# Layer 1 of a two-layer attention mixer on one core: from a scheduled loop to steps in a written order, with the range checks inside it

## The chip, the cores and the metric

The kernel runs on one core of a Trainium2 chip, in one launch. The metric is the device time of a run in microseconds (us). The profile shows one execution: its span runs from the first to the last instruction. The engines are TensorE (PE: matmuls and transposes, with weight loads as PEld), VectorE (DVE), ScalarE (ACT), GpSimd (POOL) and SyncE (SP, which issues the DMAs). They run side by side and wait for each other by semaphores. Matmuls write to PSUM[...]; ACT and DVE read them out from there, which is called evacuating a bank.

## What is computed

The input x has 128 rows of 256 tokens with 256 channels, all float32. Two layers each add an attention to x. In front of each stands a group norm over all rows. Layer 1 is the one that changes:

```
x2 = gn(x).reshape(rows, F=256, C=256)           # 128 rows
q, k, v = split(x2 @ w_in.T + b_in)              # 4 heads of 64
scores = q k^T / 8, kept where |i - j| <= 16     # a band
out = softmax(scores) v
x = x + out @ w_out.T + b_out
```

Layer 0 is an attention without a band, with 8 heads, a bias computed from z, and a gate. The fast path of the kernel leaves out the maximum in the softmax. So at the end it checks that what it relied on lies in safe ranges (the exponentials of the bias, the reciprocal sums of both layers, the mask). One number, the verdict, then decides whether a second, general path has to run. With these inputs it does not.

## The kernel before

The kernel (`fast_kernel`) works in four stages: it loads weights and z and computes the bias exponentials `eb` and the moments of x; layer 0 over 64 pairs of rows (its last output row is multiplied at about 2219 us); layer 1 over the same 64 pairs; and the checks.

Layer 1 treats a pair `p` as follows. `prep1` loads its rows (`xt`, 512 KB), adds the output bias into a second tile `xb` on POOL, transposes `xt` on PE (L1537) into PSUM and evacuates it by ACT to `xgT`. Then come four projections of 128 output channels each, two for q and two for k (L1546, evacuated by ACT), and the values of the two rows (L1560, evacuated by a DVE add). `scores1` makes the scores of one row (L1585): only the band is computed, in blocks of 64 keys by 96 queries, and these small matmuls use 64 by 64 parts of the PE array[...]. ACT takes their exponential into `e`, and POOL multiplies `e` by the band mask in two halves (L1595). `apply1` multiplies with the values and sums up with ones (L1612), in 64 by 32 parts of the array, into the four fixed banks `o_eo` and `su_eo`. Even and odd key blocks go to different banks. Two ACT copies, three DVE adds and products and a DVE reciprocal (L1617 to L1623) join them into the normalized `oT`. `finish1` multiplies by `w_out` (L1630), and a DVE add with `xb` writes the row to `yo` (L1634). At the second row of a pair `yo` goes out, and the reciprocal sums `rv` go to DRAM (`rsum1`).

All PSUM tiles of transposes, projections, values and output rows share one tag, `mm`, with two banks; the scores have one tile of two banks. Which of the two `mm` banks a tile gets is settled when the program is built.

The order of the work in layer 1 is that of a scheduler. The loop offers the work of pair `p` and, through a generator, pieces of the preparation of pair `p + 1`; the scheduler orders the instructions by its own estimates when the program is built. Layer 0 is different: there a `manual_schedule` block takes the instructions in the order in which the code issues them.

After layer 1 the checks run (L943 to L948, called from L1684 on). `check` makes three DVE passes over a tile: greater than a lower bound, less than an upper one, and a minimum. It is called for `eb` (4096 elements per partition), for the sums of layer 0 (2048) and of layer 1 (1024), both read back from DRAM, and for the mask (256). A matmul over the four results gives the verdict.

Of the kernel before, what the change touches and what calls it, by code (L numbers as in the profile page):

```python
# [9 lines left out]
F32 = mybir.dt.float32  # L10
# [763 lines left out]
def fast_kernel(  # L774
# [164 lines left out]
    ok = const.tile([P, 4], F32, name="ok")  # L939
    nc.vector.memset(ok, 1.0)  # L940

    def check(src, lo, hi, col, pool):

        n, m = src.shape
        a = pool.tile([n, m], F32, name="chk", tag="chk", bufs=1)
        nc.vector.tensor_scalar(a, src, lo, None, ALU.is_gt)
        nc.vector.scalar_tensor_tensor(a, src, hi, a, ALU.is_lt, ALU.mult)
        nc.vector.tensor_reduce(ok[:n, col : col + 1], a, AX.X, ALU.min)  # L948
# [555 lines left out]
    DH = P // H1  # L1504
    rsum1 = dram.tile([NP, H1, 2, I], F32, name="rsum1")
    with tc.tile_pool(name="l1", bufs=2) as sb, tc.tile_pool(
# [19 lines left out]
        def prep1(p, d):  # L1526
            s0 = 2 * p
            xt = sb.tile([P, 2 * NB, C], F32, name="xt1", tag="xt", bufs=3)
            nc.sync.dma_start(xt, rows(x1[s0 // GB], s0 % GB, 2))
            xb = sb.tile([P, 2 * NB, C], F32, name="xb1", tag="xb", bufs=3)  # L1530
            nc.gpsimd.tensor_tensor(xb, xt, bcast(bout_r, 1, 2 * NB), ALU.add)  # L1531
            d["xb"] = xb
            xgT = sb.tile([P, KC, N2], F32, name="xgT1", tag="xgT")
            for k in range(KC):
                ps = mm1("ps_x1")
                for t in range(2 * NB):
                    nc.tensor.transpose(ps[:, t * P : (t + 1) * P], xt[:, t, k * P : (k + 1) * P], ident)  # L1537
                nc.scalar.activation(xgT[:, k, :], ps, AF.Identity, bias=nM1[:, k : k + 1])  # L1538
            yield
            qT = sb.tile([P, KC, N2], F32, name="qT1", tag="qT")  # L1540
            kT = sb.tile([P, KC, N2], F32, name="kT1", tag="kT")
            for n, dst in ((0, qT), (1, kT)):
                for m in range(KC):
                    ps = mm1("ps_p1")
                    for k in range(KC):
                        nc.tensor.matmul(  # L1546
                            ps, w_in[:, k, n * C + m * P : n * C + (m + 1) * P], xgT[:, k, :],
                            start=(k == 0), stop=(k == KC - 1),
                        )
                    nc.scalar.activation(  # L1550
                        dst[:, m, :], ps, AF.Identity, bias=bin_c[:, n * KC + m : n * KC + m + 1]
                    )
                    yield
            v = sb.tile([P, 2, NB, C], F32, name="v1", tag="v")
            for r in range(2):
                ps = mm1("ps_v1")
                for b in range(NB):
                    t = r * NB + b
                    for k in range(KC):
                        nc.tensor.matmul(  # L1560
                            ps[:, b * C : (b + 1) * C], xgT[:, k, t * P : (t + 1) * P], w_in[:, k, 2 * C : 3 * C],
                            start=(k == 0), stop=(k == KC - 1),
                        )
                nc.vector.tensor_tensor(  # L1564
                    v[:, r, :, :], ps.rearrange("p (b c) -> p b c", b=NB), bcast(bv1_r, 1, NB), ALU.add
                )
                yield
            d.update(qT=qT, kT=kT, v=v)

# [7 lines left out]
        def scores1(d, r):  # L1577

            ps = ps_s.tile([P, 2, 512], F32, name="ps_sc1", tag="s")
            at = lambda q, c, j: ps[:, q, (c * 2 + j) * W : (c * 2 + j + 1) * W]  # L1580
            for c in range(KC):
                for k in range(NK):
                    for q in range(2):
                        rs = slice(q * D1, (q + 1) * D1)
                        nc.tensor.matmul(  # L1585
                            at(q, c, k // 2)[half(k)],
                            d["kT"][rs, c, r * I + k * KB : r * I + (k + 1) * KB],
                            d["qT"][rs, c, r * I + q0(k) : r * I + q0(k) + W],
                            start=True, stop=True,
                        )  # L1590
            e = sm.tile([P, 2, KC, NK // 2 * W], F32, name="e1", tag="e", bufs=3)
            ev = e.rearrange("p q c w -> p q (c w)")
            nc.scalar.activation(ev, ps[:, :, : KC * NK // 2 * W], AF.Exp)  # L1593
            for q in range(2):
                nc.gpsimd.tensor_tensor(  # L1595
                    e[:, q], e[:, q], bcast(bw.rearrange("p b w -> p (b w)"), 1, KC), ALU.mult
                )
            return e

        def apply1(d, r, e):  # L1600


            for a in range(3):
                for j in range(NK // 2):
                    for h in range(H1):
                        for k in (2 * j, 2 * j + 1):
                            at = slice(h * DH, (h + 1) * DH)
                            n = k % 2
                            to = o_eo[n][at, a, q0(k) : q0(k) + W] if a < 2 else su_eo[n][at, q0(k) : q0(k) + W]
                            w = (d["v"][half(k), r, j, h * D1 + a * DH : h * D1 + (a + 1) * DH] if a < 2  # L1610
                                 else ones[half(k), :DH])
                            nc.tensor.matmul(  # L1612
                                to, w, e[half(k), h % 2, h // 2, j * W : (j + 1) * W], start=True, stop=True,
                            )
            rv = d["rv"]
            odd = sm.tile([P, 3, I], F32, name="odd1", tag="odd", bufs=2)
            nc.scalar.copy(odd[:, 2, :], su_eo[1])  # L1617
            nc.scalar.copy(odd[:, :2, :], o_eo[1])  # L1618
            nc.vector.tensor_tensor(odd[:, 2, :], su_eo[0], odd[:, 2, :], ALU.add)
            nc.vector.reciprocal(rv[:, r, :], odd[:, 2, :])  # L1620
            nc.vector.tensor_tensor(odd[:, :2, :], o_eo[0], odd[:, :2, :], ALU.add)  # L1621
            oT = sb.tile([P, 2, I], F32, name="oT1", tag="oT", bufs=3)
            nc.vector.tensor_tensor(oT, odd[:, :2, :], bcast(rv[:, r, :], 1, 2), ALU.mult)  # L1623
            return oT

        def finish1(d, r, oT, yo):
            ps = mm1("ps_y1")
            for b in range(NB):
                for k in range(KC):
                    nc.tensor.matmul(  # L1630
                        ps[:, b * C : (b + 1) * C], oT[:, k, b * P : (b + 1) * P], w_out[:, k, :],
                        start=(k == 0), stop=(k == KC - 1),
                    )
            nc.vector.tensor_tensor(  # L1634
                yo[:, r * NB : (r + 1) * NB, :], ps.rearrange("p (b c) -> p b c", b=NB),
                d["xb"][:, r * NB : (r + 1) * NB, :], ALU.add,
            )

        todo1, ends1 = [], []

        def back1():
            d_, r_, es_ = todo1.pop(0)
            ends1.append((d_, r_, apply1(d_, r_, es_)))

        def end_row1():
            d_, r_, oT_ = ends1.pop(0)
            if r_ == 0:
                d_["yo"] = sb.tile([P, 2 * NB, C], F32, name="yo", tag="yo")
            finish1(d_, r_, oT_, d_["yo"])
            if r_ == 1:  # L1650
                p_ = d_["p"]
                nc.sync.dma_start(rows(out, 2 * p_, 2), d_["yo"])
                nc.sync.dma_start(
                    rsum1[p_].rearrange("q r i -> q (r i)"), d_["rv"][0:P:DH].rearrange("q r i -> q (r i)")
                )

        d = {}
        for _ in prep1(0, d):
            pass
        for p in range(NP):  # L1660
            nxt = {}
            ahead = prep1(p + 1, nxt) if p + 1 < NP else iter(())
            d.update(p=p, rv=sb.tile([P, 2, I], F32, name="rv1", tag="rv", bufs=3))
            for r in range(2):
                es = scores1(d, r)
                next(ahead, None)
                next(ahead, None)
                late = bool(ends1)
                if todo1:
                    back1()  # L1670
                next(ahead, None)
                if late:
                    end_row1()
                next(ahead, None)
                todo1.append((d, r, es))
# [87 lines left out]
```

## Time and profile before

| | us |
|---|---|
| median of three runs | 3584.51 (3583.58 to 3585.43) |
| profiled execution, whole | 3581.69 |
| its span | 3579.1 |
| first transposes of layer 1 on PE | 2241.7 |
| last out row added on DVE | 3545.6 |
| verdict written | 3571.98 |

Busy in the 200 us from 2600 on, in the middle of layer 1: PE 199.4, weight loads 132.8, DVE 92.4, ACT 70.5, POOL 59.9. The granted PE clock is full there (1.00), and the DMA engines are busy for 17%.

How to read it: a row of the timeline has the start of a group of equal instructions, its length, the engine, the line, the operation, what it writes and reads, and how many there are. The recorded end of a matmul is modelled and reaches past the start of the next one. So the price of a block of matmuls is read from the distance between the starts of two blocks. One float32 matmul shows as two records. A remark in brackets at the end of a row tells how long the engine was idle before it, and what ended this.

### The profile page before, as it was taken

The numbers are of one execution on the slowest core, as the hardware profiler recorded it, in microseconds if no ns is written. First come the engines' busy times: TensorE is split into PE (matmuls) and PEld (weight loads), VectorE is DVE, ScalarE is ACT, GpSimd is POOL, SyncE is SP. The second block draws the span as 40 slices with busy tenths as digits, with TensorE's granted clock in tenths as the row PEclk, the third lists the DMA queues.
The fourth block names the chain that finished last, engine by engine and source line by source line (L and its number), as shares of the span: only waits on it lengthen the run. The fifth ranks groups of instructions, "written<-read, shape, count | busy, mean of one in ns | idle before, by whom it ended". The sixth has DMA issues, their size and how long they took to land.

```text
span 3579.1 us, 80651 instructions
## 1 busy us (share of the span) xinstructions
PE 3355.8 (94%) x35154; PEld 2054.8 (57%) x35154; DVE 2086.4 (58%) x3412; ACT 1373.0 (38%) x1937; POOL 1812.9 (51%) x1257
## 2 busy tenths in 40 slices
PE   5666999999999999999999997999999999999995
PEld 3333555555555555555555554566666666666664
DVE  5864666666666666666666665344444444444445
ACT  2333444444444444444444442333333333333332
POOL 2355666666666666666666663223232332323221
PEclk8778999999999999999999998999999999999998
DMA  9961122212221222122212221111111111211111
GB/s 286 320 177 45 45 69 69 69 46 69 69 69 46 69 69 69 46 69 69 69 46 69 69 63 45 61 49 61 49 60 50 53 57 49 61 50 55 55 44 51
DMA packets 246811, 263.13 MB, mean 74 GB/s; under 512 B 46000, under 2 KB 212912, under 8 KB 246320
## 3 DMA queue, kind: packets, MB, share of 16 engines
q1 hardware_dynamic: 246448, 257.88, 24.6%
q8 instruction: 278, 4.55, 0.6%
q14 instruction: 85, 0.70, 0.1%
HBM read 189.02 MB, written 68.81 MB: 72 GB/s over the span
## 4 chain that ended last, share of the span: by engine, by line
PE 83%; DVE 6%; ACT 4%; DMA 3%; POOL 2%; issue 2%; SPq 1%; ACTq 0%; DVEq 0%; POOLq 0%
PE ps_p L1233 20%; PE ps_p L1546 14%; PE ps_sc L1267 8%; PE ps_ov L1298 7%; PE ps_v L1560 6%; PE ps_y L1340 6%; PE ps_y L1630 6%; PE ps_v L1248 3%; PE ps_su L1304 3%; PE ps_sc L1585 3%; PE ps_o L1612 3%; DVE xnT L1221 2%; DMA zt<-in_z_dram 2%; PE ps_x L1215 2%; ACT e L1593 1%
## 5 line engine op out<-in xcount | busy, mean ns | idle before, releaser
L1288 POOL TENSOR_TENSOR eboth<-e 128x512 f32<-128x512 f32 x512 | 639.7, 1270 | 631.5 <-DVE e L1283 631.5
L1283 DVE TENSOR_TENSOR e<-ps_sc,eb 128x1024 f32<-128x1024 f32 x512 | 603.0, 1219 | 340.4 <-ACT ps_sc L1274 249.0
L1274 ACT ACTIVATE ps_sc<-ps_sc 128x1024 f32<-128x1024 f32 x512 | 492.8, 1006 | 540.2 <-PE ps_sc L1267 536.0
L1546 PE MATMUL ps_p<-xgT,w_in 128*128 128x512 f32 x1024 | 502.2, 614 | 4.5 <-ACT xgT L1538 0.3
L1595 POOL TENSOR_TENSOR e<-e,bw 128x384 f32<-128x384 f32 x256 | 250.5, 999 | 478.3 <-ACT e L1593 478.3
L1531 POOL TENSOR_TENSOR xb<-xt,bout_r 128x1024 f32<-128x1024 f32 x64 | 150.5, 2352 | 423.6 <-DVE yo L1634 418.9
L1267 PE MATMUL ps_sc<-qT,kT 32*128 32x256 f32 x4096 | 337.0, 403 | 15.3 <-DVE xnT L1221 13.7
L1564 DVE TENSOR_TENSOR v<-ps_v,bv_r 128x512 f32<-128x512 f32 x128 | 84.5, 660 | 364.4 <-PE ps_v L1560 364.4
L1621 DVE TENSOR_TENSOR odd<-ps_o,odd 128x512 f32<-128x512 f32 x128 | 88.5, 691 | 340.3 <-ACT odd L1618 340.2
L1267 PEld LDWEIGHTS ps_sc<-qT,kT 32*128 32x128 f32 x4096 | 206.6, 184 | 129.8 <-issue 107.7
L1298 PE MATMUL ps_ov<-e,v 128*32 128x256 f32 x4096 | 274.1, 385 | 0.5 <-DVE oT L1312 0.5
L1233 PE MATMUL ps_p<-xnT,wq 128*128 128x512 f32 x512 | 255.4, 622 | 20.2 <-DVE xnT L1221 20.2
L1546 PEld LDWEIGHTS ps_p<-xgT,w_in 128*128 128x128 f32 x1024 | 179.5, 190 | 164.5 <-issue 108.2
L1233 PE MATMUL ps_p<-xgT,wg 128*128 128x512 f32 x512 | 253.9, 618 | 0.0
L1340 PE MATMUL ps_y<-wo,oT 128*128 128x256 f32 x1024 | 243.6, 381 | 7.0 <-POOL oT L1330 7.0
L1560 PE MATMUL ps_v<-w_in,xgT 128*128 128x256 f32 x1024 | 248.3, 385 | 0.0
L1340 PEld LDWEIGHTS ps_y<-wo,oT 128*128 128x128 f32 x1024 | 195.4, 191 | 87.9 <-issue 59.7
L1630 PE MATMUL ps_y<-w_out,oT 128*128 128x256 f32 x1024 | 242.3, 379 | 3.0 <-DVE oT L1623 3.0
L1248 PE MATMUL ps_v<-wv,xnT 128*128 128x256 f32 x1024 | 242.1, 379 | 0.0
L1233 PE MATMUL ps_p<-xnT,wk 128*128 128x512 f32 x512 | 240.6, 592 | 0.0
L1620 DVE RECIPROCAL rv<-odd 128x256 f32<-128x256 f32 x128 | 224.4, 1753 | 4.4
L1630 PEld LDWEIGHTS ps_y<-w_out,oT 128*128 128x128 f32 x1024 | 194.2, 190 | 56.6 <-issue 31.9
(159 smaller groups left out, 4979.8 us busy)
## 6 DMA issues: line engine op xcount, KB each, us to landing
xa<-in_x_dram SPq DMA_DIRECT2D x8, 4096.0 KB
xt<-in_x_dram SPq DMA_DIRECT2D x64, 512.0 KB
rvb<-rsum SPq DMA_DIRECT2D x256, 128.0 KB
x<-xo SPq DMA_DIRECT2D x16, 2048.0 KB
xt<-x SPq DMA_DIRECT2D x64, 512.0 KB
out_dram<-yo SPq DMA_DIRECT2D x64, 512.0 KB
rs_r<-rs_d SPq DMA_DIRECT2D x64, 256.0 KB
rs_d<-lrs SPq DMA_DIRECT2D x64, 2.0 KB
```

What stands on the lines that cost most here:

```text
L1233: nc.tensor.matmul(ps, w[:, k, m * P : (m + 1) * P], getattr(self, src)[:, k, :], start=(k == 0), stop=(k == KC - 1),)
L1248: nc.tensor.matmul(self.ps_v[:, b * C : (b + 1) * C], self.xnT[:, k, t * P : (t + 1) * P], wv[:, k, :], start=(k == 0), stop=(k == KC - 1),)
L1267: nc.tensor.matmul(self.pss[q // 2][:, q % 2, b, :], self.kT[rs, c, r * I + b * P : r * I + (b + 1) * P], self.qT[rs, c, r * I : (r + 1) * I],
L1274: nc.scalar.activation(self.pss[a], self.pss[a], AF.Exp)
L1283: nc.vector.tensor_tensor(e, pss[a], eb[:, h : h + 2], ALU.mult)
L1288: nc.gpsimd.tensor_tensor(t, es[a][:, :, 0, :], es[a][:, :, 1, :], ALU.add)
L1298: nc.tensor.matmul(ov[q * D0 : (q + 1) * D0, :], self.v[:, r, b, h * D0 : (h + 1) * D0], es[q // 2][:, q % 2, b, :], start=(b == 0), stop= ...
L1340: nc.tensor.matmul(self.ps_y[:, b * C : (b + 1) * C], self.oT[r][:, k, b * P : (b + 1) * P], wo[:, k, :], start=(k == 0), stop=(k == KC - 1),)
L1546: nc.tensor.matmul(ps, w_in[:, k, n * C + m * P : n * C + (m + 1) * P], xgT[:, k, :], start=(k == 0), stop=(k == KC - 1),)
L1560: nc.tensor.matmul(ps[:, b * C : (b + 1) * C], xgT[:, k, t * P : (t + 1) * P], w_in[:, k, 2 * C : 3 * C], start=(k == 0), stop=(k == KC - 1),)
L1595: nc.gpsimd.tensor_tensor(e[:, q], e[:, q], bcast(bw.rearrange("p b w -> p (b w)"), 1, KC), ALU.mult)
L1630: nc.tensor.matmul(ps[:, b * C : (b + 1) * C], oT[:, k, b * P : (b + 1) * P], w_out[:, k, :], start=(k == 0), stop=(k == KC - 1),)
```

## The change

Layer 1 becomes a class with steps, as layer 0 has it, and its loop stands in a `manual_schedule` block. In an iteration three pairs are at work: `was` (its second row of value products and its output rows), `now` (scores and the first row of value products) and `nxt` (projections and values); `nn` is loaded at the start and transposed at the end. Score blocks stand directly ahead of value product blocks, twice per pair.

The bias is added into `xt` itself after the transposes, so `xb` is gone; `xt` has four buffers, where both had three. The copies after the value products come in another order, sums first. The checks are cut into pieces of 512 elements per partition, one per iteration at its end. The mask and the sums of layer 0 are loaded ahead of the loop, the sums of layer 1 of the first 56 pairs in iteration 58. The `rv` of the last eight pairs are no longer written to DRAM: they are checked where they are computed. The result tile `ok` has 32 columns, and each check takes the next one. The last pair stores each row by itself.

```
-    def check(src, lo, hi, col, pool):
+    def check(src, lo, hi, pool):
+        n = src.shape[1]
+        a = pool.tile([P, 512], F32, name="chk", tag="chk", bufs=1)[:, :n]
         nc.vector.tensor_scalar(a, src, lo, None, ALU.is_gt)
         nc.vector.scalar_tensor_tensor(a, src, hi, a, ALU.is_lt, ALU.mult)
+        nc.vector.tensor_reduce(ok[:, len(done) : len(done) + 1], a, AX.X, ALU.min)
+        done.append(src)
...
+    LATE = 8
...
+            def turn(self):
+                self.xgT = sb.tile([P, KC, N2], F32, name="xgT1", tag="xgT")
+                for k in range(KC):
+                    ps = mm1("ps_x1")
+                    for t in range(2 * NB):
+                        nc.tensor.transpose(
+                            ps[:, t * P : (t + 1) * P], self.xt[:, t, k * P : (k + 1) * P], ident
+                        )
+                    nc.scalar.activation(self.xgT[:, k, :], ps, AF.Identity, bias=nM1[:, k : k + 1])
+                nc.gpsimd.tensor_tensor(self.xt, self.xt, bcast(bout_r, 1, 2 * NB), ALU.add)
...
+            def apply(self, r):
...
+                nc.scalar.copy(odd[:, 2, :], su_eo[1])
+                nc.scalar.copy(odd[:, :2, :], o_eo[1])
+                nc.vector.tensor_tensor(odd[:, 2, :], su_eo[0], odd[:, 2, :], ALU.add)
+                nc.vector.reciprocal(rv[:, r, :], odd[:, 2, :])
+                nc.vector.tensor_tensor(odd[:, :2, :], o_eo[0], odd[:, :2, :], ALU.add)
+                oT = sb.tile([P, 2, I], F32, name="oT1", tag="oT", bufs=3)
+                nc.vector.tensor_tensor(oT, odd[:, :2, :], bcast(rv[:, r, :], 1, 2), ALU.mult)
+                self.oT[r] = oT
+                if r == 1 and self.p < NP - LATE:
+                    nc.sync.dma_start(rsum1[self.p]..., rv[0:P:DH]...)
+                elif r == 1 and self.p < NP - 1:
+                    check(rv.rearrange("p r i -> p (r i)"), 1e-16, 1e8, sm)
+                elif self.p == NP - 1:
+                    check(rv[:, r, :], 1e-16, 1e8, sm)
...
+        with tc.manual_schedule():
+            was = Nobody()
+            for p in range(NP):
+                nn = pair1(p + 2)
+                if p == NP - LATE + 2:
+                    load_sums(rsum1[: NP - LATE].rearrange("n q r i -> (n q r i)"), "sums1")
+                now.scores(0)
+                was.apply(1)
+                was.out_row(0)
+                nxt.project("qT", 0)
+                nxt.project("kT", 0)
+                nxt.project("qT", 1)
+                now.scores(1)
+                now.apply(0)
+                nxt.project("kT", 1)
+                nxt.values(0)
+                nxt.values(1)
+                was.out_row(1)
+                nn.turn()
+                if checks and p > 0:
+                    checks.pop(0)()
+                was, now, nxt = now, nxt, nn
+            was.apply(1)
+            was.out_row(0)
+            was.out_row(1)
```

The other steps (`project`, `values`, `scores`, `out_row`) issue the same instructions as before.

## The prediction

> **What bounds the kernel now.** I read the page first, then stretches, waits and the timeline of single pairs of layer 1. In the page TensorE (PE) leads by far.
>
> ```profile
> PE 3355.8 (94%) x35154; PEld 2054.8 (57%) x35154; DVE 2086.4 (58%) x3412; ACT 1373.0 (38%) x1937; POOL 1812.9 (51%) x1257
> PE   5666999999999999999999997999999999999995
> ```
>
> Layer 1 fills the slices from the 27th on; there PE is busy 199.3 of every 200 us, and up to the final checks the list of waits has under 5 us for it. So a pair lasts as long as its PE blocks follow each other, and the timeline of PE (start, length, what) gives each block's price as the distance between starts. One whole pair:
>
> ```profile
> 2601.94 1.98 PE L1546 MATMUL ps_p<-xgT,w_in 128*128 128x512 f32 x4
> 2603.76 1.89 PE L1630 MATMUL ps_y<-w_out,oT 128*128 128x256 f32 x8
> 2605.48 1.88 PE L1546 MATMUL ps_p<-xgT,w_in 128*128 128x512 f32 x4
> 2607.29 0.89 PE L1585 MATMUL ps_sc<-qT,kT 64*64 64x96 f32 x32
> 2608.11 1.98 PE L1546 MATMUL ps_p<-xgT,w_in 128*128 128x512 f32 x4
> 2609.94 1.89 PE L1560 MATMUL ps_v<-w_in,xgT 128*128 128x256 f32 x8
> 2611.76 0.93 PE L1612 MATMUL ps_o<-e,v 64*32 64x96 f32 x60
> ...
> 2613.05 1.99 PE L1560 MATMUL ps_v<-w_in,xgT 128*128 128x256 f32 x8
> 2614.88 1.89 PE L1630 MATMUL ps_y<-w_out,oT 128*128 128x256 f32 x8
> 2616.70 0.89 PE L1585 MATMUL ps_sc<-qT,kT 64*64 64x96 f32 x32
> 2617.52 1.15 PE L1537 MATMUL ps_x<-ident,xt 128*128 128x128 f32 x8
> 2618.60 0.51 PE L1612 MATMUL ps_o<-e,v 64*32 64x96 f32 x18
> 2619.18 1.98 PE L1546 MATMUL ps_p<-xgT,w_in 128*128 128x512 f32 x4
> 2621.09 0.73 PE L1612 MATMUL ps_o<-e,v 64*32 64x96 f32 x40
> ```
>
> I call them S (scores), A (value products and sums), P (projection), V (values), Y (out row), X (transposes). The pair is 20.27 us. A full-array block between full ones takes 1.72 (Y at 2603.76 to 2605.48), one beside a tiled block (64*64, 64*32) 1.81 to 1.83, P between two tiled ones 1.91. So each border between full and tiled costs 0.1. There are ten per pair, and one A is cut in two: 0.58 + 1.12 where a whole one is 1.29.
>
> [...] the end of layer 1, where they already stand side by side, prices it: S 0.83, A 1.29, no more than apart.
>
> ```profile
> 3529.12 0.89 PE L1585 MATMUL ps_sc<-qT,kT 64*64 64x96 f32 x32
> 3529.95 0.93 PE L1612 MATMUL ps_o<-e,v 64*32 64x96 f32 x60
> ...
> 3531.24 1.99 PE L1630 MATMUL ps_y<-w_out,oT 128*128 128x256 f32 x8
> ```
>
> [...]
>
> **The change on PE, without waits.** As built, layer 0 keeps its instructions and their order but for one small memset. In layer 1 the new order of a pair is S A Y P P P S A P V V Y X: four borders of full and tiled, no cut A. In starts: S 0.83, A 1.29, Y 1.83, P 1.72, P 1.72, P 1.81, S 0.83, A 1.29, P 1.82, V 1.72, V 1.72, Y 1.72, X 0.98 (1.08 less one border) = 19.28. Gain 0.99 per pair.
>
> **The wait that it adds.** P, V, Y and X share two PSUM banks (tag mm). In before, S or A stands between many of these blocks and covers their evacuation. The new order puts four and six in a row. As built, the waits of PE in one pair of the changed kernel are:
>
> ```
> L1649 Matmult ps_y [waits Activation]
> L1562 Matmult ps_p (q, m=0) [waits Activation]
> L1562 Matmult ps_p (k, m=0) [waits Activation]
> L1562 Matmult ps_p (q, m=1) [waits DVE]
> ...
> L1550 Matmult ps_x (k=0) [waits DMA, DVE]
> L1550 Matmult ps_x (k=1) [waits DVE]
> ```
>
> In the built program k's first projection has the bank of q's first, directly before it, in every full pair; the second transpose group has the bank of the Y just before X. The prices:
>
> - k after q: ACT starts an evacuation 1.92 to 1.98 after the start of its P, takes 0.69, PE follows 0.05 later (as in the ramp shown below, where the DVE add ended 2273.51 and PE went on at 2273.56). A restarted block has its weight load exposed: 0.08 (the last Y, which waited, starts 3543.59, its DVE add 3545.60, 2.01 against 1.93 in stream). 1.95 + 0.69 + 0.05 + 0.08 - 1.72 = 1.05 of idle PE.
> - x1 after Y: DVE starts 1.93 after Y's start (2609.94 to 2611.86 for V of that shape), 0.68, 0.05: 2.66. PE would be there at 1.72 + 0.435 = 2.16. With 0.05 for the weights: 0.55.
>
> The same wait is seen once in before, in the ramp:
>
> ```profile
> 2273.56 0.66 PE L1537 MATMUL ps_x<-ident,xt 128*128 128x128 f32 x4 [0.36 <-DVE v L1564]
> ```
>
> So 1.60 of waiting against 0.99 of gain: the pair is 20.88, 0.61 longer. Behind a waiting block stand all later blocks of PE; ACT, DVE and POOL then only run later by as much. Other evacuations fit: q's second projection needs Y's DVE add. Behind A, counted from its end, the DVE queue is su add 0.63, reciprocal 1.08, o add 2.75, oT 3.48, Y's add 4.09, done 4.78; q comes at 6.3. Their lengths:
>
> ```profile
> 2602.90 0.41 DVE L1619 TENSOR_TENSOR odd<-ps_su,odd 128x256 f32<-128x256 f32 x1
> 2603.35 1.75 DVE L1620 RECIPROCAL rv<-odd 128x256 f32<-128x256 f32 x1
> 2605.14 0.69 DVE L1623 TENSOR_TENSOR oT<-odd,rv 128x512 f32<-128x512 f32 x1
> ```
>
> The second Y of a pair needs the V add at 4.8 and comes at 5.3. exp (0.81) and two POOL products (1.0 each) after S have 9 us and more before their A. POOL's in-place add (2.35, formerly xb) comes after X, before the products of the next S; those are not due for 8 us. On SP the next xt load stands behind the out store of the pair before, 18 us before its X; a 512 KB load landed in under 4.2 (2237.48 to 2241.70).
>
> **The checks.** A piece of 512 is 0.43 + 0.69 + 0.69 = 1.8 us (between the 256 and 1024 rows: 293/425/420 ns and 693/1225/1221). Fifteen pieces stand at the end of pairs behind the last Y add, where DVE has 3 us until A's chain: nothing, and if that cover were gone 27 us at most. The loads of mask (128 KB) and sums (1 MB) stand on SP ahead of xt of pair 2, due 30 us later: nothing. The last pairs' rv is checked in A's own chain instead of stored (one DMA less): Y's add is then done at 6.6, and q's second projection waits 0.42 (pairs 57 to 62).
>
> **The end.** In before 3545.60 (last add) to 3571.98 (verdict) is checks, then 7.1 to the span's end. After: from the end of the A in the last pair, DVE sets the pace: chain 4.1, check 1.8, add 0.6; next chain from 6.5, its o add at 9.3 frees ps_o for the last A (9.4 to 10.7); check 1.2, add to 11.8; last chain to 15.3, last Y 15.4, its add at 17.4, verdict at 18.2. The 7.1 stay; the last store (3 us) runs within them.
>
> **Sum**, from the end of the prologue's V (2256.4): pair 0 16.3; 56 pairs 56 x 20.88 = 1169.3; five with a check 5 x 21.30 = 106.5; pair 62, without X, 19.9; pair 63 2.1 and the end 18.2. That is 1332.3. In before it is 3571.98 - 2256.4 = 1315.6. The profiled execution, 3581.7 with a span of 3579.1, becomes 16.7 longer; the median shown is 2.8 above it, so 3584.5 + 16.7 = 3601. A difference under 0.2% (7 us) a measurement here cannot tell from none.
>
> **Rivals.**
> 1. No bank waits (the claim of the change taken at its word): 61 x 1.60 = 98 less: 3503. Against: the built waits and the 0.36 in the ramp. 4%.
> 2. One of the two is covered: without x1's 3601 - 34 = 3567, without k's 3601 - 64 = 3537. The change is faster once both sum to under 1.2 per pair, slower above 1.44; between lies no change. Nothing in before shows a P evacuated faster than 1.92 + 0.69, so 4%.
> 3. The k projection waits for DVE, as a strict rotation of two banks would have it: Y's add 4.78 + 0.13 against 3.55: 1.36, so 61 x 0.31 = 19 more: 3620. The built wait speaks against. 7%.
> 4. S beside A saves nothing in a stream (0.1 on four borders returns): 24 more, 3625. The end of before speaks against it. 5%.
> 5. The forecast itself, 80%: restart and ACT start are each known to 0.05 to 0.1, which is 3 to 6 us over 61 pairs each; the ends to 4. That gives 3587 to 3613 as its own range; its low edge, one in eight, lies within 0.2%.
>
> Slower 0.82, same 0.10, faster 0.08. The range 3586 to 3618 leaves out rivals 1, 2, 4 and part of 3.
>
> **What would show it.** PE in layer 1 at some 92% instead of 99.6; waits of ps_p for ACT (about 60 of 1 us) and of ps_x for DVE y (about 60 of 0.5); S and A together 2.12; the tail's DVE at a few microseconds. It is wrong if the pair is under 20.6 or over 21.2, or if q's second projection waits in all pairs.

## The result, and the profile after

The changed kernel takes 3597.01 us (median of four, 3595.68 to 3597.88) against 3584.05 for the kernel before on the same chip: a ratio of 1.0038, 95% interval 1.0021 to 1.0055. In a later comparison on another occasion it was 3599.72 against 3583.15, 1.0045 (1.0032 to 1.0059). So it is slower by 13 to 17 us. The forecast was 3601 with a range of 3586 to 3618. The profiled executions are 3596.1 us of span after and 3579.1 before, 17.0 apart; 16.7 was worked out.

From the page of the changed kernel: busy time by engine, and PE in forty slices of the span.

```profile
PE 3330.5 (93%) x35154; PEld 2059.5 (57%) x35154; DVE 2114.0 (59%) x3471; ACT 1387.5 (39%) x1937; POOL 1815.3 (50%) x1257
PE   5666999999999999999999996999999999999998
```

PE does the same 35154 records' work and is recorded 25 us less busy in a span that is 17 us longer. The slices can't show where: a slice of layer 1 is still over 90% busy. The list of PE's waits between 2300 and 3560 us shows it (for whom, sum in us, times, longest):

```profile
PE ps_p L1562 <- ACT qT L1566: 47.5, 61, 0.8
PE ps_x L1550 <- DVE yo L1653: 20.9, 60, 0.3
```

Two waits, once per pair each. The timeline of PE places them in a pair (start, length, line, operation, shape; in brackets the idle time before the row):

```profile
2607.55 0.89 PE L1593 MATMUL ps_sc<-qT,kT 64*64 64x96 f32 x32
2608.38 0.93 PE L1621 MATMUL ps_o<-e,v 64*32 64x96 f32 x60
...
2609.67 1.99 PE L1649 MATMUL ps_y<-w_out,oT 128*128 128x256 f32 x8
2611.50 1.88 PE L1562 MATMUL ps_p<-xgT,w_in 128*128 128x512 f32 x4
2614.16 3.70 PE L1562 MATMUL ps_p<-xgT,w_in 128*128 128x512 f32 x8 [0.78 <-ACT qT L1566]
2617.79 0.89 PE L1593 MATMUL ps_sc<-qT,kT 64*64 64x96 f32 x32
...
2625.18 1.89 PE L1649 MATMUL ps_y<-w_out,oT 128*128 128x256 f32 x8
2626.90 0.60 PE L1550 MATMUL ps_x<-ident,xt 128*128 128x128 f32 x4
2627.85 0.66 PE L1550 MATMUL ps_x<-ident,xt 128*128 128x128 f32 x4 [0.35 <-DVE yo L1653]
2628.43 0.89 PE L1593 MATMUL ps_sc<-qT,kT 64*64 64x96 f32 x32
```

From S to the S of the next pair it is 2628.43 - 2607.55 = 20.88, the length worked out. S and A stand together and take 2.12, as at the end of before. The gain of the fewer borders and the uncut A is there, and the two waits take more than it. Their releasers end just before PE goes on: ACT's evacuation of q runs from 2613.42 to 2614.11, and DVE's add for the out row from 2627.10 to 2627.79. The cost of the waits is larger than the idle time that the profile writes, since the recorded end of a matmul reaches past the next start (q's block is recorded with 1.88 and takes 1.72 between starts). By starts, k follows q after 2.66 where an undisturbed block takes 1.72 (0.94), and k and q's second projection together take 3.63 instead of 3.53 (0.10, the restart; PE's weight loads begin together with the block there, at 2614.16, and 0.22 ahead of it in a row of full blocks, 2624.96 for the out row at 2625.18): 1.04. The second transposes follow the first after 0.95 instead of 0.435, and S follows 0.045 later than it would: 0.56. The pair less both, 20.88 - 1.60, is the 19.28 of the prediction's sum.

### The profile page after: what moved, and what is told of

Same layout as the page of the kernel before. It is cut to its first block, busy times and chain, and to the rows that moved or that the text cites. A ratio compares the mean times of both kernels' runs of the same rounds, so it can differ in the third digit from the quotient of the medians.

```text
span 3596.1 us, 80678 instructions
## 1 busy us (share of the span) xinstructions
PE 3330.5 (93%) x35154; PEld 2059.5 (57%) x35154; DVE 2114.0 (59%) x3471; ACT 1387.5 (39%) x1937; POOL 1815.3 (50%) x1257
## 4 chain that ended last, share of the span: by engine, by line
PE 84%; DVE 6%; ACT 3%; DMA 2%; POOL 2%; issue 2%; SPq 1%; DVEq 0%; POOLq 0%; ACTq 0%
PE ps_p L1234 20%; PE ps_p L1562 13%; PE ps_sc L1268 8%; PE ps_ov L1299 7%; PE ps_y L1649 6%; PE ps_v L1577 6%; PE ps_y L1341 6%; PE ps_o L1621 3%; PE ps_v L1249 3%; PE ps_su L1305 3%; PE ps_sc L1593 3%; DVE xnT L1222 2%; PE ps_x L1216 2%; DMA zt<-in_z_dram 2%; PE ps_su L1621 1%
## 5 line engine op out<-in xcount | busy, mean ns | idle before, releaser
L1562 PE MATMUL ps_p<-xgT,w_in 128*128 128x512 f32 x1024 | 485.7, 607 | 48.4 <-ACT qT L1566 48.3
L1630 DVE TENSOR_TENSOR odd<-ps_su,odd 128x256 f32<-128x256 f32 x128 | 54.3, 424 | 560.0 <-ACT odd L1628 560.0
L1554 POOL TENSOR_TENSOR xt<-xt,bout_r 128x1024 f32<-128x1024 f32 x64 | 153.8, 2403 | 445.0 <-PE ps_x L1550 445.0
L1649 PE MATMUL ps_y<-w_out,oT 128*128 128x256 f32 x1024 | 250.4, 388 | 0.9 <-DVE oT L1634 0.9
L1577 PE MATMUL ps_v<-w_in,xgT 128*128 128x256 f32 x1024 | 231.4, 379 | 0.0
L1553 ACT ACTIVATE xgT<-ps_x,nM 128x512 f32<-128x512 f32 x128 | 88.0, 688 | 369.0 <-PE ps_x L1550 327.0
L1577 PEld LDWEIGHTS ps_v<-w_in,xgT 128*128 128x128 f32 x1024 | 194.6, 190 | 53.8 <-issue 30.6
```

The lines of the kernel that those rows point to most:

```text
L1562: nc.tensor.matmul(ps, w_in[:, k, n * C + m * P : n * C + (m + 1) * P], self.xgT[:, k, :], start=(k == 0), stop=(k == KC - 1),)
L1577: nc.tensor.matmul(ps[:, b * C : (b + 1) * C], self.xgT[:, k, t * P : (t + 1) * P], w_in[:, k, 2 * C : 3 * C], start=(k == 0), stop=(k == ...
L1649: nc.tensor.matmul(ps[:, b * C : (b + 1) * C], self.oT[r][:, k, b * P : (b + 1) * P], w_out[:, k, :], start=(k == 0), stop=(k == KC - 1),)
```

## The experiments

All times are in us. Line numbers are those of the variant, which shift by two where `turn` is split. "The changed kernel" is the one of the result.

**The out row between q and k.** The two tiles that the k projection and the first one of q put into the same bank get a third block between them.

```
                 was.apply(1)
-                was.out_row(0)
                 nxt.project("qT", 0)
+                was.out_row(0)
                 nxt.project("kT", 0)
```

> The changed kernel with two steps swapped: the output row of the pair before goes between q's first and k's first projection (S A P Y P P). Theory (bank waits): k's first projection no longer follows the tile in its own bank, the Y covers the evacuation; q's second needs Y's DVE add 4.9 us after A and comes at 5.3. Pairs of 20.88 become 19.84; in the last pairs q's second projection gets the bank of the k just before it and waits 1.0 there. 3597 - 56 x 1.04 - 6 x 0.4 = 3536. Rival (idle PE comes from the row of four full blocks itself, or from data and not from the bank): pair stays 20.88, 3597. Rival (the DVE add of Y is the real limit): the wait moves to q's second projection, 3597 or a little above.

Measured: 3539.91, ratio to before 0.9876 (0.986 to 0.9893). The full pair is 19.83. The list of PE's waits of this variant, from 2300 us up to the last pair:

```profile
PE ps_x L1550 <- DVE yo L1653: 20.9, 60, 0.3
PE ps_p L1562 <- ACT kT L1566: 5.0, 6, 0.8
```

The wait for q's evacuation is gone and the wait of the transposes is as it was. So the first wait alone is worth 57 us, and without it this kernel is faster than before. The second line is the wait that was foreseen for the six pairs at the end, which carry a range check in the chain behind A: there q's second projection waits, and the full ones among them last 20.93. Against the 21.11 of the changed kernel that is a gain of 0.18 each, where 0.4 had been reckoned: 1.3 of the 4 us that the expectation missed. Another 1.0 lies ahead of the first score block, which starts at 2258.47 here and at 2257.49 in the changed kernel; the rest is open. The list names ACT rightly: as built, this projection has k's bank in these pairs, directly behind it, where it has the out row's in all others. Why the bank differs there is not shown; it fits that with the checks elsewhere, below, the choice is the usual one again. The choice hardly matters in size: k's evacuation ends 3435.27 and PE goes on at 3435.32 in one of them, the out row's add ends 3435.43.

**The transposes apart.** The two halves of `turn` go to other places, each beside a tiled block, and the order is otherwise that of the changed kernel. `turn` takes the halves that it has to do, and POOL's add of the bias stays with the second.

```
                 nxt.project("qT", 1)
+                nn.turn([0])
                 now.scores(1)
                 now.apply(0)
+                nn.turn([1])
                 nxt.project("kT", 1)
...
-                nn.turn()
```

> The changed kernel with the two transpose groups apart: the first behind q's second projection, the second behind the second value product block, so that S and A stand between them. Nothing else is moved. Theory (bank waits): the second group no longer waits for Y's DVE add, 0.56 per pair less; number of borders the same. Pair 20.32, 3597 - 61 x 0.56 = 3563, and ps_x waits for DVE yo are gone while the k projection still waits 0.8 to 1.0 for ACT. Rival: the 0.35 idle is a cost of transposes behind full blocks: 3597.

Measured: 3562.58, ratio 0.9941 (0.9924 to 0.9958); the full pair is 20.27. Up to the last pair PE's only wait is now the first one:

```profile
PE ps_p L1564 <- ACT qT L1568: 47.5, 61, 0.8
```

The second wait alone is worth 34 us. The pair is 0.61 shorter, though, where the wait was 0.56. The other 0.05 comes with the new place: the two halves, each beside one tiled block, take 0.53 and 0.50, where X in one piece between two tiled blocks took 1.08 in before.

**Both.**

```
                 was.apply(1)
-                was.out_row(0)
                 nxt.project("qT", 0)
+                was.out_row(0)
                 nxt.project("kT", 0)
                 nxt.project("qT", 1)
+                nn.turn([0])
                 now.scores(1)
                 now.apply(0)
+                nn.turn([1])
...
-                nn.turn()
```

> Both edits together: S A P Y P P X | S A X P V V Y. Theory: all waits of a full pair are gone and what is left is the sum of PE starts, 19.27 per pair: 3597 - 56 x 1.60 - 5 x 1.0 - 1 = 3502, faster than before by 2.3%. Rival (four and six full blocks in a row leave some limit anyway, such as DVE's queue): the pair stays above 19.8 and the time above 3535.

Measured: 3501.15, ratio 0.9769 (0.9753 to 0.9785). The full pair is 19.22. Here PE is recorded busy for 200.0 of the 200 us from 2600 on, and up to 3480 us only the wait of the pairs at the end is left (besides one of 0.6 for the value products of the end):

```profile
PE ps_p L1564 <- ACT kT L1568: 5.0, 6, 0.8
```

The second half of a pair, from X to the next S, whose predecessor had started at 2600.27:

```profile
2612.01 0.65 PE L1551 MATMUL ps_x<-ident,xt 128*128 128x128 f32 x4
2612.50 1.88 PE L1564 MATMUL ps_p<-xgT,w_in 128*128 128x512 f32 x4
2614.22 3.62 PE L1579 MATMUL ps_v<-w_in,xgT 128*128 128x256 f32 x16
2617.67 1.89 PE L1651 MATMUL ps_y<-w_out,oT 128*128 128x256 f32 x8
2619.49 0.89 PE L1595 MATMUL ps_sc<-qT,kT 64*64 64x96 f32 x32
```

So without the waits the fewer borders and the uncut A give what the prediction's sum promised: 20.27 to 19.22. That is 1.05 per pair where the prediction had 0.99; 0.05 of it comes with the place of the transposes, as above.

**The checks at the end.** The loop of the changed kernel, with the range checks of before: in one piece each, behind layer 1, with all reciprocal sums stored and read back.

```
-                if r == 1 and self.p < NP - LATE:
+                if r == 1:
                     nc.sync.dma_start(rsum1[self.p]...)
...
-                if checks and p > 0:
-                    checks.pop(0)()
```

> The changed kernel with the checks as before: whole tiles after layer 1, every pair's sums stored. Only the order of layer 1 is then new. Theory: the loop's pair stays 20.88; the tail from the last add to the verdict is 26.4 again instead of 0.75 (+25.6), the late pairs lose their wait of 0.42 (-2.5) and the last chains their checks (-4.5): 3597 + 19 = 3616, so the order alone costs 32 against before. Rival (the pieces in the loop cost time in 13 pairs, up to 1.8 each): the gain of moving them is only 19 - 24, 3592.

Measured: 3621.76, ratio 1.0105 (1.0089 to 1.0122), 6 above the number expected. All its full pairs are 20.88 and its two waits are those of the changed kernel. Its last add starts at 3584.92 and its verdict at 3610.34, 25.4 later; in before these are 3545.60 and 3571.83, 26.2. So the order alone costs 39.3 up to the last add, and moving the checks into the loop gives 21.6 back (spans 3617.7 and 3596.1). The changed kernel is the sum of a loss and a gain, of which the loss is the larger.

**Two banks strictly in turn.** This puts rival 3 of the prediction into effect: k's first projection shares its bank with the out row before q.

```
+        turns = [0]
         def mm1(name):
-            return ps_mm.tile([P, 512], F32, name=name, tag="mm")
+            turns[0] += 1
+            return ps_mm.tile([P, 512], F32, name=name, tag=f"mm{turns[0] % 2}", bufs=1)
```

> The order of the changed kernel, but its mm tiles take the two banks strictly in turn, so that k's first projection has the bank of the out row before q and waits for DVE's add there, no longer for ACT's evacuation of q; the second transposes keep the bank of the out row before them. Theory (which bank a tile has decides whom PE waits for): the distance from q to k plus k to q1 grows from the 6.29 of the changed kernel to about 6.6 (1.36 of idle PE in place of 1.04), the pair is 21.2 us against 20.88, the list of waits shows ps_p waiting for DVE yo in about 60 pairs and none for ACT qT; about 3616 us. Rival (the four full blocks behind each other cost the same whatever the banks, for instance by weight loads): pair 20.88 and 3597 as the changed kernel. If the add comes earlier than I think, below 3597.

Measured: 3626.47, ratio 1.0124 (1.0107 to 1.0141). The timeline of PE:

```profile
2614.07 1.88 PE L1564 MATMUL ps_p<-xgT,w_in 128*128 128x512 f32 x4
2616.89 3.70 PE L1564 MATMUL ps_p<-xgT,w_in 128*128 128x512 f32 x8 [0.94 <-DVE yo L1655]
```

The add that releases it, on DVE:

```profile
2616.15 0.68 DVE L1655 TENSOR_TENSOR yo<-ps_y,xt 128x512 f32<-128x512 f32 x1
```

And the line of the list of waits (2300 to 3600 us):

```profile
PE ps_p L1564 <- DVE yo L1655: 68.0, 61, 2.7
```

The name of the engine that PE waits for has changed with the bank, in every pair, and nothing in the order of the blocks has. Full blocks in a row cost nothing of themselves: with both edits five stand together, X P V V Y, and P and each V take 1.72 to 1.73. By size I was wrong twice. The wait is 2616.89 - 2614.07 - 1.72 = 1.10 by starts, 1.20 with the 0.10 of the restart, instead of 1.36. So the pair is 0.16 longer than in the changed kernel, 21.04 and not 21.2. And the late pairs last 22.8 to 24.5: there the check, 1.8 on DVE, stands ahead of the add that k waits for, and comes on top in full; in four of them the granted clock fell too (last section). These six pairs make 16.5 us more than in the changed kernel, the 56 others 9.

**One more pair of borders.** The version with both edits, and the second transposes between S and A.

```
                 now.scores(1)
-                now.apply(0)
                 nn.turn([1])
+                now.apply(0)
```

> The version with the out row between q and k and the transposes apart (3501.2 us), with the second transposes put between the scores and the value products of one row instead of behind the latter. Nothing waits in either; only two more borders of full and tiled stand in each pair. Theory (a border costs 0.1, S beside A none): pair 19.22 + 0.2 = 19.42, 63 pairs, 3501.2 + 12 = 3513. Rival (the gain of the new order has another source than the borders): 3501. [...]

Measured: 3513.59, ratio 0.9806 (0.979 to 0.9822). The pair is 19.42, and nothing waits that did not wait without the edit. In the timeline of PE the second half of X stands between two tiled blocks:

```profile
2612.87 0.60 PE L1551 MATMUL ps_x<-ident,xt 128*128 128x128 f32 x4
2613.40 0.89 PE L1595 MATMUL ps_sc<-qT,kT 64*64 64x96 f32 x32
2614.22 0.66 PE L1551 MATMUL ps_x<-ident,xt 128*128 128x128 f32 x4
2614.81 0.93 PE L1623 MATMUL ps_o<-e,v 64*32 64x96 f32 x60
```

It takes 2614.81 - 2614.22 = 0.59, where it took 0.49 between A and a projection; and that projection, now beside A, takes 1.82 instead of 1.72. 12.4 us over 63 pairs are 0.20 per pair, two borders at 0.1. This is the price from which the prediction took its gain, and rival 4 falls with it: S beside A costs nothing that can be measured. S takes 0.82 (2613.40 to 2614.22) here, ahead of X, and 0.82 in the version with both edits (2620.31 - 2619.49), ahead of A.

**The late checks, first attempt.** From here on the base is the version with both edits (3501.15). The checks of `rv` of the pairs 56 to 62 leave the chain behind A and go to the end of the iteration.

```
                 elif r == 1 and self.p < NP - 1:
-                    check(rv.rearrange("p r i -> p (r i)"), 1e-16, 1e8, sm)
+                    checks.append(lambda: check(rv.rearrange("p r i -> p (r i)"), 1e-16, 1e8, sm))
...
+                while checks and p > NP - LATE:
+                    checks.pop(0)()
```

> The same version of 3501.2 us, with the range checks of rv of pairs 56 to 62 moved from the chain behind the value products to the end of the iteration, behind the last add of an out row. Theory (the check in A's chain delays the out row's add and with it the evacuation that q's second projection waits for): the waits of ps_p for ACT kT or DVE in the last pairs are gone (five of 0.8), and DVE's tail loses about a microsecond: 3501.2 - 5 - 1 = 3495. Rival (the waits of the late pairs come from the loads and not from the checks): 3500.

Measured: 3499.84, ratio 0.9768 (0.9752 to 0.9785): a fifth of the gain that I expected. The six waits of 0.8 are gone (as built, q's second projection has the out row's bank again), but one pair grew from 20.33 to 24.58. In it three pieces, two of the sums and one of `rv`, stand behind each other on DVE from 3388.90 to 3395.00, ahead of the chain of the next A. A row of PE's timeline and a stretch of the windows view (the window, its length, PE's busy time, then PEld, DVE, ACT and POOL, the granted clock, DMA) show what this did:

```profile
3399.12 3.48 PE L1564 MATMUL ps_p<-xgT,w_in 128*128 128x512 f32 x4 [3.40 <-DVE yo L1655]
```

```profile
3399.12:3402.60 3.48, 3.48 (x5) 1.39 (x6) 0.00 (x0) 0.00 (x0) 0.00 (x0) 0.55 0.00 0
```

PE waited 3.40 and then did a block of 1.72 in 3.27 (the next block starts at 3402.39), with a granted clock of 0.55; in the 15 us before the wait it was 1.00.

**The late checks, spread.** All pieces go behind the add of the first out row, where DVE has a gap, at most two per iteration.

```
                 was.out_row(0)
+                for _ in range(2):
+                    if checks and p > 0:
+                        checks.pop(0)()
                 nxt.project("kT", 0)
...
-                if checks and p > 0:
-                    checks.pop(0)()
```

> As the run with the late checks at the end of the iteration (3499.8 us), but all pieces of the range checks stand behind the add of the first out row of an iteration, where DVE is free for some 5.5 us, at most two per iteration. There three pieces in one iteration held DVE for 5.7 us, made the next chain late and PE idle for 3.4, after which a block ran slow; that pair took 24.58 instead of 19.22. Theory (only the place on DVE matters, the checks are free in its gap): every full pair 19.22, no wait of PE above 1 us before the last pair, 3499.8 - 5.4 = 3494.5. Rival (the load of the sums is what makes that pair late): it stays long and the time is 3500.

Measured: 3494.62, ratio 0.9752 (0.9738 to 0.9767). Every pair from the second to the 62nd is 19.22 or 19.23, and up to 3460 us the list of PE's waits is empty. On DVE the gap behind the out row's add, which starts at 3394.54 in one of the last pairs, holds two pieces and still leaves 1.85:

```profile
3395.14 0.41 DVE L946 TENSOR_SCALAR chk<-rv 128x512 f32<-128x512 f32 x1
...
3398.23 0.69 DVE L948 TENSOR_REDUCE ok<-chk 128x1 f32<-128x512 f32 x1
3400.76 0.42 DVE L1632 TENSOR_TENSOR odd<-ps_su,odd 128x256 f32<-128x256 f32 x1 [1.85 <-ACT odd L1630]
```

This version beats both kernels: 2.5% under before, with the steps and the pieces of the checks of the change, but another order of three of the steps and another place for the checks.

**The changed kernel again.**

> The changed kernel itself once more, beside more runs of before. The spans say 17.0 us between the two (3596.1 against 3579.1), the medians 13.0. If before's profiled execution lies low by chance and its typical span is longer, the difference of medians stays at 13 and the profiled difference of 17 was scatter; if the medians were scatter, it comes out at 16 to 17. Theory: 13 (ratio 1.0037), since the profile of before was one of its faster executions by 2.4 to 2.8 us.

Measured: 3599.72 (3599.05 to 3600.44, five runs), 16.6 above before's 3583.15. I had expected 13. All pairs are those of the result to 0.06. Of the 1.2 between the spans of the two profiled executions of the changed kernel (3597.3 and 3596.1), 1.05 lies ahead of its first score block (2258.54 against 2257.49). From the one occasion to the other the changed kernel's median moved by 2.7 and before's by 0.9; no run shows why, and 13 to 17 is as close as these runs come.

## Why the prediction was right

**The sum of blocks.** The pair without waits was put at 19.28. The changed kernel's 20.88 less its two measured waits is 19.28; the first experiment's 19.83 less the wait that it keeps is 19.27; the version without waits has 19.22, 0.06 less, since its transposes stand elsewhere. The border's 0.1 is confirmed by the run that added two. The uncut A (1.29, against 0.58 + 1.12 in before) and the S beside A at no cost are read from the timeline; no run puts the cut back.

**The two waits.** That k waits for ACT and the second transposes for DVE was read from the built program, not from the profile of before, where one such wait occurs. The k wait was priced 1.05 and is 1.04; the transposes' 0.55 and is 0.56. Undone alone they give 57 and 34 us, against 64 and 34 by the prediction's rival 2; most of the missing 7 are the six late pairs, which wait for another thing as soon as k doesn't and gain 0.18 each instead of 1.05. That a wait of PE delays all its later blocks, and that an evacuation stands behind what its engine was given before, was the author's assumption in the prediction. What was measured agrees with it: the pair is 20.88, longer than the sum of 19.28 by the whole 1.60, and in a late pair of the strict rotation the out row's add starts 2.39 after the oT product (3506.84 and 3504.45) with the three passes of the check between them, where it follows after 0.61 in the others (2616.15 and 2615.54).

In the changed order k's first projection follows q's first into the same bank and pays 1.04 per pair. But the same order with the two banks strictly in turn pays 1.20 and is slower still, 3626 against 3597 to 3600. And with both edits, where nothing waits, the tiles of the full pairs take the two banks strictly in turn too, as built. So turning the banks is not what decides here. It is how much PE work lies between a tile and the next user of its bank, set against how late the evacuation is done: from q's start 1.72 against 2.66 in the changed kernel.

**The terms that were off** nearly cancel, which is luck; but none is over 1.1. The start of the first S is 1.1 later than assumed. Pair 0 lasts 15.93 (16.3 foreseen), pair 62 19.67 (19.9). The five late pairs last 21.11 instead of 21.30: the wait of q's second projection is 0.23, not 0.42. What is at fault in it is the count of DVE's queue "behind A", which I had done at 4.78; in the strict rotation the add ends 4.59 after the out row's start. The same 0.2 is most of what made rival 3's price too high.

**The end** was put at 18.2 from the last A of pair 62 to the verdict, and is 19.3 (3570.09 to 3589.35). The check of 512 that was to take 1.8 there took 3.3; its first two passes ran beside a product on POOL.

**What would show it** had one number wrong. PE was to be at some 92% in layer 1; between 2600 and 2800 it is recorded busy for 189.5 of 200, 94.8%. I worked out the share from starts and forgot that recorded ends cover part of a wait: the same reason for which the list says 0.8 and 0.3 where 1 and 0.5 were announced. The verdict on the theory was right all the same because the pair's length, 20.88, is a distance of starts.

**The step from the profiled execution to the median** held within what the runs scatter: the 16.7 came back as 17.0 in the spans, 13.0 in the first medians and 16.6 in the second.

## What to carry to other kernels

When instructions are put into a new order, list for each PSUM tile which block uses its bank next, and compare the PE time between the two with the evacuation (when it starts, how long it takes, and how long PE then needs to go on); where that PE time is shorter, PE pays the difference in every round (1.04 and 0.56 per pair here), and one swap of two steps can take it away (57 us here). Small gains per border, 0.1 here, are real and add up, but they are smaller than one such wait. Work that is "free" on an engine with slack is free only in the gap between two chains: by its place in the queue one check cost between nothing and 1.8 us per pair here, and three of them in a row 5.4.

## What I had not expected of the hardware

**VectorE beside GpSimd.** In the version with both edits the product that makes `oT` takes twice its time in one of two rows, namely where POOL adds the bias (DVE's rows, and POOL's in the second fence):

```profile
2615.31 1.33 DVE L1636 TENSOR_TENSOR oT<-odd,rv 128x512 f32<-128x512 f32 x1
...
2624.91 0.69 DVE L1636 TENSOR_TENSOR oT<-odd,rv 128x512 f32<-128x512 f32 x1
```

```profile
2613.74 2.36 POOL L1556 TENSOR_TENSOR xt<-xt,bout_r 128x1024 f32<-128x1024 f32 x1
```

The POOL add ends at 2616.10, and 0.54 later the product is done. In the run with one more pair of borders the same add ends at 2619.60, only 0.19 after the product has started; the product takes 0.74 and is done 0.55 after the add. In the changed kernel, where the two do not overlap, it takes 0.69 in both rows. The reciprocal, with one input, takes its 1.75 (from 2612.98) beside POOL's work too, the products that end at 2613.78 and then the add. In the end of the changed kernel the first two passes of the check take 1.23 and 1.37 (from 3574.01 and 3575.27) instead of 0.42 and 0.69; POOL's products run there from 3573.95 to 3576.09. That is 1.5 more, against an excess of that end of 1.1. The first of them has one SBUF input only, like the reciprocal, which is not slowed; what decides it is not shown by these runs. In the loop the slow product costs nothing: DVE has slack behind it (0.63 idle ahead of the second V add), and the pair is 19.22.

**The clock after a wait.** After a wait of 3.40 the granted clock was 0.55 in the next block, as above. In the strict rotation it was lower after waits of 2.72 (2.88 by starts) in four of six late pairs: in one of them k and q's second projection take 5.02 instead of 3.63, at a granted clock of 0.72. In the other two, with the same wait, it stayed up: 3.63 at 1.00. So these runs show a fall after 3.40 (3.56 by starts) and after some waits of 2.72, and no run here shows why it is in four cases and not in two. The short waits of the changed kernel, up to 1, cost no clock: it is 1.00 from 2614.16 to 2617.79, behind the first of them, and over the stretch from 2300 to 3500.
